# The end of a streamed cross attention: weighted sums, denominators and value biases in another order and on another engine

## The chip, the cores and the metric

The kernel runs on one core of a Trainium2 chip. The metric is the device time of one execution in microseconds. Before the change the median of three runs is 1160.88 us (1160.07 to 1163.15).

## What is computed

One block of a perceiver, all in float32 at its inputs and outputs: 512 tokens `x` of 512 numbers attend to 8192 context vectors, then to each other by linear attention, and then go through a feed-forward layer in simulated 8-bit arithmetic. Each part is added to `x`.

```python
def reference(x, ctx_1024, ...):
    # cross attention: 16 heads of 32, softmax over 8192 keys
    q = split_heads(layernorm(x) @ Wq + bq)
    k = split_heads(ctx_1024 @ Wk + bk)
    v = split_heads(ctx_1024 @ Wv + bv)
    z = softmax(q k^T / sqrt(32)) v
    x = x + merge_heads(z) @ Wo + bo
    # linear attention: 128 random features per head, elu + 1
    x = x + _L0_attn_ref(layernorm(x), w_qkv, proj_matrix, w_out, b_out)
    # feed-forward: 8-bit quantized products, exact gelu between
    x = x + _L0_ffn_ref(layernorm(x), W1, b1, W2, b2)
    return x
```

The change concerns the cross attention alone: the weighted sums of `v`, the denominators of the softmax, and the value bias `bv`, which is added after the division, since the weights of a softmax sum to 1.

## The kernel before

**Tiling.** The 8192 keys are taken in 16 blocks of 512. Heads are taken four at a time, so that four heads of 32 numbers fill 128 partitions; there are four such groups `g`. A block has four tiles `k` of 128 keys. A unit is one triple (block, g, k), and the loop at L784 goes through all 256 of them, in this order, 16 per block: the last block's are the units from `last_block` (240) on. They are numbered 0 to 15 below; unit 4 is the first of group 1, and so on.

**A unit's work.** `weights` (L723) makes the scores of four heads against 128 keys, four products on TensorE into `sc`, which takes four PSUM banks and has one buffer, and then the exponentials `ex` (128 x 2048) on ScalarE; `ex` has four buffers. So the scores of the next unit wait until ScalarE has read the last ones. `summed` (L748) adds the exponentials to a running sum `acc[:, g]` on VectorE, from which the denominators come at the very end. `weighted_sums` (L679) multiplies a unit's exponentials with the values, into a PSUM tile `av` which collects the four units of a group; the function that it returns adds that tile to `Z[:, g]` on VectorE after the fourth (L696), and does nothing after the others. The weighted sums run late: `late` holds the units whose exponentials are made and whose weighted sums are not.

**What else TensorE does.** Keys and values of the next block are made in small steps, kept in `queue` and issued by `ahead` between the units. In the last block what is left are keys of that block's own later groups (`pk`, L395), one product per unit, as long as there are any (to unit 10); their results get their bias on ScalarE (L401).

**The last block before the change** (L786 to L804). After a unit's scores and exponentials, VectorE gets the unit's addition to the running sum. In the second unit of a group (`k == 1`) the group before is finished (`finish`, L717): its denominators `dn` are a product of the running sum with ones (`sums`, L700), VectorE takes their reciprocal (`inverse`, L707), multiplies Z with it and adds the value bias (`divide`, L710). Then come the weighted sums of the unit before with their addition to Z, and then a step of the queue. Group 3's denominators are collected in another tile over its four units straight from the exponentials, and group 3's running sum gets no additions in this block. `av` and `dn` share two PSUM buffers (`ps_a`), which are handed on as they come free.

**Order.** Nearly every instruction goes through `in_order`, which keeps it in the program's order on its engine. Each engine takes its instructions one after the other, so an instruction that waits holds all behind it on that engine; engines wait for each other by semaphores.

**Behind the block** the output products `po` (L840) multiply Z with `Wo`, token tile by token tile: first groups 0 to 2 for two tiles, then group 3. Normalization, linear attention and the feed-forward layer follow.

Of the kernel before, what the change touches and what calls it, by code (L numbers as in the profile page):

```python
# [9 lines left out]
F32 = mybir.dt.float32  # L10
BF16 = mybir.dt.bfloat16
AF = mybir.ActivationFunctionType
ALU = mybir.AluOpType
# [4 lines left out]
P = 128  # L18
# [9 lines left out]
def network(  # L28
# [24 lines left out]
    nc = tc.nc  # L53
    S, E = x.shape
# [4 lines left out]
    NE = E // P  # L59
# [32 lines left out]
    def in_order(i):  # L92

        return tc.keep_in_program_order(i)
# [6 lines left out]
    def load_cols(src, n, name):  # L101
        t = const.tile([P, n], F32, name=name)
        nc.sync.dma_start(t, src)
        return t
# [6 lines left out]
    def place_w():  # L111
        return wpool.tile([P, NE, E], F32, name="w")

    def load_w(src, w=None):
        w = w or place_w()
        nc.sync.dma_start(w, src.rearrange("(c p) n -> p c n", p=P))
        return w
# [146 lines left out]
    with ExitStack() as actx:  # L264
# [5 lines left out]
        Z = aw.tile([P, NE, S], F32, name="Z")  # L270
        acc = aw.tile([P, NE, HG, S], F32, name="acc")
# [7 lines left out]
        bias = aw.tile([P, NE], F32, name="bias")  # L279

        rd = acc[:, :, 0, :]
# [28 lines left out]
        bv_sb = load_cols(bv, NE, "bv_sb")  # L310
# [238 lines left out]
        def ahead(n):  # L549
            for _ in range(n):  # L550
                cost, step = queue.pop(0)
                step()
                done[0] += cost
# [120 lines left out]
        ps_a = ctx.enter_context(tc.tile_pool(name="ps_a", bufs=2, space=PSUM))  # L674
        sctx = actx.enter_context(ExitStack())
        ps_s = sctx.enter_context(tc.tile_pool(name="ps_s", bufs=1, space=PSUM))
        av, late = {}, []

        def weighted_sums(b, g, k, ex):  # L679
            if k == 0:  # L680
                av[g] = ps_a.tile([P, S], F32, name="av")
            assert ("v", b, k, g // 2) in made
            for j in range(HG):
                in_order(nc.tensor.matmul(  # L684
                    av[g][ts(j, D), :], lhsT=vt[b][:, k, ds(g * P + j * D, D)],
                    rhs=ex[:, j, :], start=(k == 0), stop=(k == NC - 1),
                ))
            if k < NC - 1:
                return lambda: None
            ps = av.pop(g)  # L690

            def added():
                if b == first:
                    in_order(nc.vector.tensor_copy(Z[:, g, :], ps))
                else:
                    in_order(nc.vector.tensor_tensor(Z[:, g, :], Z[:, g, :], ps, ALU.add))  # L696

            return added

        def sums(dn, ex, start, stop):  # L700
            for j in range(HG):
                in_order(nc.tensor.matmul(
                    dn[ts(j, D), :], lhsT=ones_f, rhs=ex[:, j, :],
                    start=start, stop=stop,
                ))

        def inverse(g, dn):  # L707
            in_order(nc.vector.reciprocal(rd[:, g, :], dn))

        def divide(g):  # L710

            in_order(nc.vector.tensor_tensor(Z[:, g, :], Z[:, g, :], rd[:, g, :], ALU.mult))
            in_order(nc.vector.tensor_scalar(
                Z[:, g, :], Z[:, g, :], bv_sb[:, g : g + 1], None, ALU.add
            ))

        def finish(g):  # L717
            dn = ps_a.tile([P, S], F32, name="dn", tag="av")
            sums(dn, acc[:, g], True, True)
            inverse(g, dn)  # L720
            divide(g)

        def weights(b, g, k):  # L723

            assert ("k", b, g, k // 2) in made
            sc = ps_s.tile([P, HG, S], F32, name="sc")
            if exact:
                for j in range(HG):
                    in_order(nc.tensor.matmul(
                        sc[:, j, :], lhsT=ones_h[ds(j * D, 3), :],  # L730
                        rhs=mrow[ds(j * D, 3), g, :], start=True, stop=False,
                    ))
            for j in range(HG):
                rows = ts(j, D)
                in_order(nc.tensor.matmul(  # L735
                    sc[:, j, :], lhsT=kT[b][rows, g, ts(k, P)], rhs=qT[rows, g, :],
                    start=not exact, stop=True,
                ))
            ex = ap4.tile([P, HG, S], F32, name="ex")
            if exact:  # L740
                in_order(nc.scalar.activation(ex, sc, AF.Exp, scale=SCALE))
            else:
                in_order(nc.scalar.activation(  # L743
                    ex, sc, AF.Exp, bias=bias[:, g : g + 1], scale=SCALE
                ))
            return ex

        def summed(b, g, k, ex):  # L748
            if b == first and k == 0:
                in_order(nc.vector.tensor_copy(acc[:, g], ex))  # L750
            elif (b, g) != (total - 1, NE - 1):
                in_order(nc.vector.tensor_tensor(acc[:, g], acc[:, g], ex, ALU.add))  # L752
# [23 lines left out]
        def due(i):  # L776
            for (i0, c0), (i1, c1) in zip(marks, marks[1:]):
                if i <= i1:
                    return c0 + (c1 - c0) * (i - i0) // (i1 - i0)
            return c1  # L780
# [3 lines left out]
        for i, u in enumerate(units):  # L784
            ex = weights(*u)
            if i >= last_block:  # L786
                b, g, k = u
                summed(*u, ex)
                if k == 1 and g > 0:
                    finish(g - 1)  # L790
                if g == NE - 1:
                    if k == 0:
                        dn = ps_m.tile([P, S], F32, name="dn", tag="pt")
                    sums(dn, acc[:, g] if k == 0 else late[0][-1], k == 0, False)
                while late:
                    weighted_sums(*late.pop(0))()
                if queue:
                    ahead(1)
                if i == last_block + 2:

                    wo_sb, wv2_sb = load_w(Wo), place_w()
                    wk2_sb = load_w(w_qkv[:, E : 2 * E])
                    wq2_sb = load_w(w_qkv[:, :E])
                    load_w(w_qkv[:, 2 * E :], wv2_sb)  # L804
            elif i % 3 == 0 and i > 0:
                add = [weighted_sums(*late.pop(0)) for _ in range(3)]
                summed(*u, ex)
                for a in add:
                    a()
                if wq_steps:  # L810
                    wq_steps.pop(0)()
            else:
                upto = due(i + 1) if i % 3 == 2 else (due(i - 1) + due(i + 2)) // 2
                if i < 3:
                    upto = done[0] + 4
                while queue and done[0] < upto:
                    ahead(1)
                summed(*u, ex)
            late.append((*u, ex))
# [3 lines left out]
        inverse(NE - 1, dn)  # L823
        weighted_sums(*late.pop(0))()
        divide(NE - 1)

# [384 lines left out]
    for q in range(NF // 4):  # L1213
# [14 lines left out]
        for i in range(4):  # L1228
# [7 lines left out]
            if i % 2 == 1:  # L1236
                k = f // 2
# [49 lines left out]
@with_exitstack  # L1287
def perceiver_block(ctx: ExitStack, tc: tile.TileContext, **args):
    nc = tc.nc
    fate = ctx.enter_context(tc.tile_pool(name="fate", bufs=1))  # L1290
    wrong = fate.tile([1, 1], mybir.dt.int32, name="wrong")
    network(tc, False, wrong, **args)
    again = nc.values_load(wrong, min_val=0, max_val=1)
    with tc.If(again > 0):
        network(tc, True, None, **args)
# [50 lines left out]
```

## Time and profile before

| | us |
|---|---|
| median of three runs | 1160.88 |
| the profiled execution | 1161.99 |
| its span | 1160.1 |
| TensorE busy in the span | 1102.5 |
| VectorE busy | 929.6 |
| ScalarE busy | 630.7 |
| last block, from its first scores to the first output product | 936.93 to 996.11 |
| exponentials of one unit (L743), mean | 1.968 |
| reciprocal of 128x512 (L708), mean | 3.355 |
| value bias on VectorE (L713), mean | 0.487 |
| key bias on ScalarE (L401), mean | 0.688 |

The times of the profile count from the start of the span. PE is TensorE, PEld its weight loads, DVE VectorE, ACT ScalarE, SP the engine that issues most transfers. Matmuls are pipelined, so the length printed for one is longer than the distance from its start to the next one's; distances of starts say what it costs. The granted clock of TensorE is 1.00 in the whole last block.

### The profile page before, as it was taken

What the parts mean: (1) busy time and instruction counts of PE and PEld (TensorE: products, weight loads), DVE (VectorE), ACT (ScalarE), POOL (GpSimd) and SP (SyncE); (2) the same over time, 40 slices, a digit from 0 to 9 for tenths busy, and PEclk for the clock granted to TensorE, in tenths of its full rate; (3) what the DMA queues carried; (4) which work ended last, traced back from release to release, by engine and by line L of the source; (5) the groups of instructions that cost most, each with busy time, mean ns of one, the idle gap of its engine ahead of it and who ended that gap; (6) DMA issues with size and microseconds to landing.
All of it is one profiled execution on the core that took longest, in us unless ns stands there. A gap on an engine that the chain in (4) does not pass through costs nothing.

```text
span 1160.1 us, 15823 instructions
## 1 busy us (share of the span) xinstructions
PE 1102.5 (95%) x6793; PEld 524.5 (45%) x6793; DVE 929.6 (80%) x840; ACT 630.7 (54%) x419; POOL 138.0 (12%) x80
## 2 busy tenths in 40 slices
PE   5999999999999999999999999999999999999865
PEld 2334454444544544544544544545544422344332
DVE  2458899989888888888888888888888879656886
ACT  1044555456666666666665555555555565336353
POOL 2420203003203011203010202010100000000000
PEclk9999999999999999999999999999999999999987
DMA  7021212120202120202110101010100021030001
GB/s 254 1 73 44 85 55 73 55 81 13 89 29 67 53 64 28 91 28 64 55 46 10 37 1 38 1 37 1 37 37 1 1 74 37 37 146 1 1 1 39
DMA packets 24686, 54.59 MB, mean 47 GB/s; under 512 B 1952, under 2 KB 2464, under 8 KB 24352
## 3 DMA queue, kind: packets, MB, share of 16 engines
q1 hardware_dynamic: 24320, 52.97, 13.8%
q8 instruction: 55, 0.90, 0.3%
q10 hardware_dynamic: 288, 0.52, 0.1%
q14 instruction: 23, 0.19, 0.1%
HBM read 48.25 MB, written 5.24 MB: 46 GB/s over the span
## 4 chain that ended last, share of the span: by engine, by line
PE 83%; DVE 8%; issue 5%; ACT 4%; POOL 0%; DVEq 0%; POOLq 0%; ACTq 0%
PE pm L467 29%; PE sc L735 22%; PE av L684 18%; ACT ex L743 4%; DVE acc L752 2%; PE pk L395 2%; PE po L840 2%; PE pq L944 2%; PE pys L1253 1%; PE pq L122 1%; PE pv L876 1%; DVE unchanged L129 1%; PE pv L417 1%; DVE de L1044 1%; PE att L1034 1%
## 5 line engine op out<-in xcount | busy, mean ns | idle before, releaser
L743 ACT ACTIVATE ex<-sc,bias 128x2048 f32<-128x2048 f32 x256 | 503.8, 1968 | 406.0 <-PE sc L735 400.2
L752 DVE TENSOR_TENSOR acc<-acc,ex 128x2048 f32<-128x2048 f32 x248 | 587.0, 2368 | 78.1 <-ACT ex L743 75.9
L735 PE MATMUL sc<-qT,kT 32*128 32x512 f32 x2048 | 292.0, 640 | 5.3 <-ACT ex L743 4.8
L684 PE MATMUL av<-ex,vt 128*32 128x512 f32 x2048 | 239.5, 596 | 1.6 <-DVE Z L696 1.6
L735 PEld LDWEIGHTS sc<-qT,kT 32*128 32x128 f32 x2048 | 79.9, 182 | 140.6 <-ACT ex L743 124.4
L684 PEld LDWEIGHTS av<-ex,vt 128*32 128x32 f32 x2048 | 57.2, 109 | 169.6 <-issue 166.2
L380 POOL TENSOR_TENSOR tt<-ct 128x512 f32<-128x512 f32 x30 | 47.7, 1591 | 614.0 <-DMA ct<-in_ctxT 606.8
L467 PE MATMUL pm<-w,tt 128*128 128x256 f32 x480 | 118.3, 389 | 0.3 <-ACT vt L488 0.3
L467 PE MATMUL pm<-tt,w 128*128 128x256 f32 x448 | 110.5, 389 | 0.2 <-DVE kT L478 0.2
L467 PEld LDWEIGHTS pm<-w,tt 128*128 128x128 f32 x480 | 87.4, 190 | 44.8 <-issue 31.0
L467 PEld LDWEIGHTS pm<-tt,w 128*128 128x128 f32 x448 | 81.5, 190 | 42.5 <-issue 26.4
L475 DVE TENSOR_TENSOR vt<-vt,pm 128x512 f32<-128x512 f32 x105 | 70.6, 685 | 30.1 <-PE pm L467 22.3
L467 PE MATMUL pm<-w,ct 128*128 128x256 f32 x360 | 91.8, 391 | 0.0
L467 PE MATMUL pm<-ct,w 128*128 128x256 f32 x336 | 85.6, 391 | 4.9 <-DVE kT L478 3.9
L467 PEld LDWEIGHTS pm<-w,ct 128*128 128x128 f32 x360 | 65.0, 189 | 36.4 <-issue 29.2
L467 PEld LDWEIGHTS pm<-ct,w 128*128 128x128 f32 x336 | 60.7, 189 | 38.4 <-issue 25.5
L380 POOL TENSOR_TENSOR tt<-ct,tt 128x512 f32<-128x512 f32 x30 | 75.2, 2508 | 1.2
L475 DVE TENSOR_TENSOR kT<-kT,pm 128x512 f32<-128x512 f32 x56 | 38.2, 682 | 15.0 <-PE pm L467 9.2
L478 DVE SCALAR_TENSOR_TENSOR kT<-pm,bk_sb,kT 128x256 f32<-128x256 f32 x84 | 36.5, 476 | 5.5 <-PE pm L467 5.2
L696 DVE TENSOR_TENSOR Z<-Z,av 128x512 f32<-128x512 f32 x60 | 40.8, 679 | 0.0
L966 ACT ACTIVATE er<-feat 128x1024 f32<-128x1024 f32 x32 | 30.2, 1028 | 8.9 <-PE feat L987 6.7
L970 DVE SCALAR_TENSOR_TENSOR f<-er 128x1024 f32<-128x1024 f32 x16 | 19.4, 1219 | 15.1 <-ACT er L966 15.1
(172 smaller groups left out, 598.3 us busy)
## 6 DMA issues: line engine op xcount, KB each, us to landing
ct<-in_ctxT SPq DMA_DIRECT2D x16, 1024.0 KB, 5.7
wraw<-in_W1T SPq DMA_DIRECT2D x16, 512.0 KB, 3.8
wraw<-in_W2T SPq DMA_DIRECT2D x16, 512.0 KB, 3.6
wd<-wquant SPq DMA_DIRECT2D x16, 256.0 KB, 2.4
w_q<-wd SPq DMA_DIRECT2D x2, 2048.0 KB, 10.6
w<-in_w_qkv SPq DMA_DIRECT2D x3, 1024.0 KB, 5.1
w<-in_Wq SPq DMA_DIRECT2D x1, 1024.0 KB, 8.4
w<-in_Wk SPq DMA_DIRECT2D x1, 1024.0 KB, 10.2
```

Source lines behind the costliest of these rows:

```text
L380: in_order(nc.gpsimd.tensor_tensor(tt[b][:, i], x, y, ALU.subtract))
L395: in_order(nc.tensor.matmul(part[0], lhsT=wk_sb[:, c, ts(g, P)], rhs=ct[b][:, c, :], start=(c == 0), stop=(c == NE - 1),))
L467: in_order(nc.tensor.matmul(st["ps"][n][:, m, :], lhsT=lhsT[:, k, ts(m, P)], rhs=rhs[:, k, :], start=k == 0, stop=k == 1,))
L475: in_order(nc.vector.tensor_tensor(dst, src, ps, ALU.add))
L478: in_order(nc.vector.scalar_tensor_tensor(dst[:, m, :], ps[:, m, :], bk_sb[:, 2 * i + m : 2 * i + m + 1], src[:, m, :], ALU.add, ALU.add,))
L684: in_order(nc.tensor.matmul(av[g][ts(j, D), :], lhsT=vt[b][:, k, ds(g * P + j * D, D)], rhs=ex[:, j, :], start=(k == 0), stop=(k == NC - 1),))
L696: in_order(nc.vector.tensor_tensor(Z[:, g, :], Z[:, g, :], ps, ALU.add))
L735: in_order(nc.tensor.matmul(sc[:, j, :], lhsT=kT[b][rows, g, ts(k, P)], rhs=qT[rows, g, :], start=not exact, stop=True,))
L743: in_order(nc.scalar.activation(ex, sc, AF.Exp, bias=bias[:, g : g + 1], scale=SCALE))
L752: in_order(nc.vector.tensor_tensor(acc[:, g], acc[:, g], ex, ALU.add))
L840: in_order(nc.tensor.matmul(po, lhsT=lhsT[:, c, ts(t, P)], rhs=w[:, c, :], start=(c == 0), stop=(c == NE - 1),))
L966: in_order(nc.scalar.activation(er[-1][:, d].rearrange("p a n -> p (a n)"), ps[h], function))
```

## The change

It has three parts, all in the last block.

- The weighted sums of the unit before, with their addition to Z, and the step of the queue now come ahead of the unit's addition to the running sum. On TensorE nothing but their place against the denominators changes by it; on VectorE an addition to Z stands ahead of a running sum behind which it stood.
- The denominators of the group before come behind the unit's weighted sums and its step of the queue, no longer ahead of them. The reciprocal and the multiplication follow the unit's running sum on VectorE, as before.
- The value bias is taken out of `divide` into a new function `biased`. For groups 0 to 2 it is issued in the fourth unit of the next group and runs on ScalarE, as an activation with the identity function; for group 3 it stays on VectorE, behind the multiplication.

```diff
         def divide(g):
-
             in_order(nc.vector.tensor_tensor(Z[:, g, :], Z[:, g, :], rd[:, g, :], ALU.mult))
-            in_order(nc.vector.tensor_scalar(
-                Z[:, g, :], Z[:, g, :], bv_sb[:, g : g + 1], None, ALU.add
-            ))
-
-        def finish(g):
-            dn = ps_a.tile([P, S], F32, name="dn", tag="av")
-            sums(dn, acc[:, g], True, True)
-            inverse(g, dn)
-            divide(g)
+
+        def biased(g):
+
+            if g < NE - 1:
+                in_order(nc.scalar.activation(
+                    Z[:, g, :], Z[:, g, :], AF.Identity, bias=bv_sb[:, g : g + 1]
+                ))
+            else:
+                in_order(nc.vector.tensor_scalar(
+                    Z[:, g, :], Z[:, g, :], bv_sb[:, g : g + 1], None, ALU.add
+                ))
...
             if i >= last_block:
                 b, g, k = u
-                summed(*u, ex)
-                if k == 1 and g > 0:
-                    finish(g - 1)
+
+
                 if g == NE - 1:
...
                     weighted_sums(*late.pop(0))()
                 if queue:
                     ahead(1)
+                if k == 1 and g > 0:
+                    dn_g = ps_a.tile([P, S], F32, name="dn", tag="av")
+                    sums(dn_g, acc[:, g - 1], True, True)
+                summed(*u, ex)
+                if k == 1 and g > 0:
+                    inverse(g - 1, dn_g)
+                    divide(g - 1)
+                if k == 3 and g > 0:
+                    biased(g - 1)
...
         inverse(NE - 1, dn)
         weighted_sums(*late.pop(0))()
         divide(NE - 1)
+        biased(NE - 1)
```

## The prediction, made before the changed kernel had run

> **What bounds the kernel now.** I read the page's busy shares first, then the chain that ended last, then the waits of the last block alone, and at the end the timeline of that block, engine by engine. The block's sixteen units are numbered 0 to 15 here, four to a group; unit 0's scores start at 936.93 us, and the output products behind the block start at 996.11 us.
>
> ```profile
> PE 1102.5 (95%) x6793; PEld 524.5 (45%) x6793; DVE 929.6 (80%) x840; ACT 630.7 (54%) x419; POOL 138.0 (12%) x80
> PE 83%; DVE 8%; issue 5%; ACT 4%; POOL 0%; DVEq 0%; POOLq 0%; ACTq 0%
> ```
>
> TensorE is busy 95% of the span and is 83% of the chain: what takes it work or waiting off is worth time one for one, and what is done for the other engines is worth nothing unless TensorE or the loop scores - exponentials - scores waits for it. The change touches only the last 60 us before the output products, so these decide. The chain in order of time, units 4 to 6 (start, length, what):
>
> ```profile
> 951.46 1.18 PE sc L735 x8
> 952.64 0.02 issue
> 952.66 1.98 ACT ex L743
> 954.64 0.02 issue
> 954.66 2.29 DVE acc L752
> 956.96 0.61 DVE Z L696
> 957.57 0.04 issue
> 957.61 1.07 PE av L684 x8
> 958.68 1.06 PE pk L395 x2
> 959.73 1.07 PE sc L735 x8
> ```
>
> In unit 5 the chain leaves TensorE: it goes through the exponentials of unit 4, their running sum and the addition of group 0's weighted sums to Z, and only then do the weighted sums of group 1 start. It does the same at 969.33 to 972.28 (unit 9). The same stretch in the timeline:
>
> ```profile
> 954.68 1.14 PE L735 MATMUL sc<-qT,kT 32*128 32x512 f32 x8
> 955.76 1.07 PE L702 MATMUL dn<-acc,ones_f 128*32 128x512 f32 x8
> 957.61 1.07 PE L684 MATMUL av<-ex,vt 128*32 128x512 f32 x8 [0.79 <-DVE Z L696]
> 958.61 1.13 PE L395 MATMUL pk<-ct,w 128*128 128x512 f32 x2
> 959.66 1.14 PE L735 MATMUL sc<-qT,kT 32*128 32x512 f32 x8
> 960.10 3.35 DVE L708 RECIPROCAL acc<-dn 128x512 f32<-128x512 f32 x1
> 960.87 1.97 ACT L743 ACTIVATE ex<-sc,bias 128x2048 f32<-128x2048 f32 x1 [3.01 <-PE sc L735]
> 963.49 0.69 DVE L712 TENSOR_TENSOR Z<-Z,acc 128x512 f32<-128x512 f32 x1
> 964.22 0.49 DVE L713 TENSOR_SCALAR Z<-Z,bv_sb 128x512 f32<-128x512 f32 x1
> ```
>
> An ordinary unit takes 3.23 us from scores to scores (962.89, 966.12, 969.35): 1.21 us from the scores' start to the exponentials', 1.97 us of exponentials, 0.04 us to the next scores. Unit 5 takes 4.98 us (954.68 to 959.66), unit 9 too (969.35 to 974.33), unit 13 takes 3.79 us (984.02 to 987.80). The waits of the block put 1.6 us in two pieces of 0.8 us to the addition to Z.
>
> **The change part by part.** *Additions to Z ahead of the running sums.* Group 0's last weighted sums start at 952.53 us (unit 4) and VectorE's running sum before them ends at about 953.73, so the addition can run 953.75 to 954.43 instead of 956.87 to 957.55, and unit 4's running sum, ready at 954.63, still starts on time. In group 1 it stands behind the sums of units 6 and 7, as before, and comes at about 968.9 to 969.6; nobody on TensorE hangs on that one at the weighted sums any more: by the order of buffers in the changed program the weighted sums of group 1 take a PSUM buffer free since unit 0, those of group 2 the one that the reciprocal of group 0 left (963.45), and only the denominators of group 1, three products later (about 971.7), wait for that addition. Both 0.79 us waits go. In unit 0, the addition now waits for three units' weighted sums (to about 940.8) and the running sum slips from 940.14 to about 941.5, ending 943.8; the next one starts when its exponentials end (944.95), which hides it.
>
> *Denominators behind the unit's other products.* Unit 5 becomes scores, weighted sums, keys, denominators, scores. Start to start, from rows: scores to 128x32 products 1.07 us (945.00 to 946.07), those to keys 1.00 us (957.61 to 958.61), keys to whatever follows 1.06 us (973.27 to 974.33), 128x32 products to scores 0.97 us (986.83 to 987.80). Sum 4.10 us against 4.98: 0.88 us less. The unseen step is keys to denominators; its nearest row is keys to scores (1.05 to 1.12 us), and the last step lies between 0.87 (denominators on denominators) and 1.0 us, so 3.99 to 4.20 us. The old order without its wait would be 4.98 - 0.85 = 4.13 us by starts, or about 4.0 us by pitches: the new order itself gains nothing. Twice 0.88 us: 1.76 us (1.56 to 1.98). In unit 13 there is no keys' product left and no wait before: 1.07 + 0.87 + 0.87 + 0.97 = 3.78 us against 3.79, no gain. The reciprocal of group 2 starts at TensorE's pace, 1.1 us after its denominators, so later within the unit; VectorE has nothing else there (idle 1.66 us before it now), and Z of group 2 is wanted only in the third output product.
>
> [...]
>
> *Three bias additions on ScalarE.* VectorE loses 3 x 0.49 us (L713). Its additions to Z no longer hold TensorE, so the time it saves is worth 0; if they still did, group 1's bias alone would be on the path, 0.4 us. ScalarE gets three. The nearest rows, the same operation with PSUM as source (L401, L346), take 0.69 us; a 128x1024 one in SBUF (L211) takes 1.23 us, which bounds it from above. They stand behind the exponentials of units 7, 11 and 15. There ScalarE waits 1.26 us for the next scores, which hides 0.69 us; the upper bound leaves 0.03. What they bring is a wait: they need VectorE's product with the reciprocal, and the next exponentials queue behind them. That product ends at 964.18 us for group 0 (nothing before it moves); unit 7's exponentials end at about 965.2 and unit 8's start at 966.45, so it could be 1.6 us later. For group 1, VectorE runs the sums of units 6 and 7 (from 964.22, 2.39 us apart), the addition (968.9), the sums of 8 and 9 (969.6, 971.9), the reciprocal (974.1) and the product (977.5 to 978.2); unit 12's exponentials start at 980.3 us: 1.4 us to spare. The third lies behind the last exponentials, ahead of the table load, whose function is wanted 10 us later. Cost 0.
>
> [...]
>
> *A by-product.* In the changed program four exponentials (units 8, 9, 12, 13) wait for the scores in a separate instruction ahead of them, as they now know of VectorE's sums through the bias. The nearest row is the addition to xs (L846): the one with such a wait starts 0.11 us after its product's end (1002.50), the one without 0.04 us (1010.15). I take 0.07 us, 0 to 0.1. It counts only where ScalarE's loop sets the pace, units 8 and 12: 0.14 us.
>
> *Behind the block* the order is the old one, and neither SP's nor GpSimd's queue changes. The last weight load (977.55, released by the last keys' product) moves up with it; the output products, normalizations and the rest are released by TensorE and VectorE and shift as a whole.
>
> Sum: 1.76 - 0.14 = 1.62 us. The profiled execution took 1161.99 us (span 1160.1 and 1.9 around it), so 1160.4; it is 1.1 us above the median of the runs shown, 1160.88, from which I predict 1159.3 us. By the bounds of the parts the gain is 1.4 to 2.0 us, 1158.9 to 1159.5.
>
> **The rivals.** *The gain does not reach the end* (1160.9). From 1090 us on, TensorE is idle by stretches (busy 0.74 of 5 us at 1100, none at 1125) and the granted clock falls to 0.50 at 1105 and 1130 to 1140. Where the fall lies against the stages is not set by this block; 1.6 us more of the tail at half clock costs 0.8 us, as much less saves it, and both such places together could take the gain. For it: the three runs shown lie 3.1 us apart. Against: nothing in the chain behind 996 us has a fixed date.
>
> *ScalarE waits for VectorE* (slower). The place is the bias after units 7 and 11. From 1.6 and 1.4 us of lateness of VectorE on, each further us delays the next exponentials by one. One running sum (2.29 us) more ahead of each reciprocal costs 0.7 + 0.9 us and just eats the gain (1160.9); it decides from about 2.3 us on, and two sums (4.58 us) cost 3.0 + 3.2 us: 1165.5. For it: VectorE is busy 14.1 of 14.67 us in units 5 to 8. Against: it loses a bias per group, and the product's date follows from rows.
>
> *TensorE packs tighter.* If the denominators fit beside the exponentials, units 5, 9 and 13 take 3.23 us: 3 x 3.23 against 4.98 + 4.98 + 3.79 gives 4.1 us less, 1156.8. Against: four products at 0.87 us or more already take 3.5.
>
> **How the numbers follow.** My forecast has 0.75, the lost gain 0.12, ScalarE's wait 0.07 (0.05 of it past the bound), the tighter packing 0.06. Some 0.3% (3.5 us) is what a measurement here can tell from no change: the forecast (0.14%) and the lost gain are the same by it. Faster by more: the tighter packing and a lucky tail, 0.08; slower 0.05; the same 0.87. The range goes from the tighter packing, 1157.0, over the forecast and the lost gain with 1 us of scatter on it, to 1161.9.
>
> **What would show it.** Right: in unit 5 and unit 9 no wait of the weighted sums for Z, scores 4.1 us apart; the bias on ScalarE at 0.6 to 0.75 us in a gap before unit 8 and unit 12; output products at about 994.5 us. Wrong: exponentials of unit 8 or 12 released by VectorE's product, denominators waiting for the addition to Z, or the span not following the output products' start.

## The result and the profile after

The changed kernel is faster by 0.16%: the ratio of its runs to those of the kernel before is 0.9984, with a 95% interval of 0.9976 to 0.9992 (12 runs each; medians 1160.2 and 1161.5 us). In a later comparison, beside other experiments, it was 0.9978 (0.9969 to 0.9987). In microseconds that is a gain of 1.9 (0.9 to 2.8) and 2.6 (1.5 to 3.6); the forecast was 1.6. The forecast time, 1159.3 us, counted from the 1160.88 us of three runs; over twelve runs the kernel before has a median of 1161.5 us.

The page of the changed kernel, busy shares and the chain's shares by engine:

```profile
PE 1101.9 (95%) x6790; PEld 523.9 (45%) x6793; DVE 926.1 (80%) x837; ACT 632.5 (55%) x422; POOL 138.2 (12%) x80
PE 84%; DVE 7%; ACT 4%; issue 4%; POOL 0%; DVEq 0%; ACTq 0%; POOLq 0%
```

TensorE's work is the same; one per cent of the chain went from VectorE to TensorE. The chain in order of time, units 4 to 6, as it was shown of the kernel before:

```profile
949.98 1.14 PE sc L736 x8
951.12 1.00 PE av L684 x8
952.11 1.06 PE pk L395 x2
953.17 0.04 issue
953.20 1.14 PE sc L736 x8
954.35 0.99 PE av L684 x8
955.34 1.06 PE pk L395 x2
956.40 1.00 PE dn L702 x8
957.39 1.07 PE sc L736 x8
```

The chain no longer leaves TensorE in unit 5: exponentials, running sum and addition to Z are gone from it. The timeline of the changed kernel over the same stretch follows; in brackets stands how long the engine was idle ahead of a row, and what ended that (`<-`):

```profile
952.18 0.69 DVE L696 TENSOR_TENSOR Z<-Z,av 128x512 f32<-128x512 f32 x1
953.18 2.29 DVE L753 TENSOR_TENSOR acc<-acc,ex 128x2048 f32<-128x2048 f32 x1 [0.32 <-ACT ex L744]
...
953.20 1.14 PE L736 MATMUL sc<-qT,kT 32*128 32x512 f32 x8
954.27 1.06 PE L684 MATMUL av<-ex,vt 128*32 128x512 f32 x8
955.27 1.12 PE L395 MATMUL pk<-ct,w 128*128 128x512 f32 x2
956.33 1.06 PE L702 MATMUL dn<-acc,ones_f 128*32 128x512 f32 x8
957.32 1.14 PE L736 MATMUL sc<-qT,kT 32*128 32x512 f32 x8
...
962.00 0.69 DVE L711 TENSOR_TENSOR Z<-Z,acc 128x512 f32<-128x512 f32 x1
...
963.62 0.71 ACT L716 ACTIVATE Z<-Z,bv_sb 128x512 f32<-128x512 f32 x1
965.05 1.97 ACT L744 ACTIVATE ex<-sc,bias 128x2048 f32<-128x2048 f32 x1 [0.71 <-PE sc L736]
```

The addition to Z ends at 952.87 us, ahead of the running sum of unit 4, which still starts 0.03 us after its exponentials, as before the change. Weighted sums, keys and denominators follow each other without a wait, and unit 5 takes 4.12 us from scores to scores instead of 4.98. The bias on ScalarE finds its operand 0.9 us early and is done 0.7 us before the next exponentials.

What the bias brings to these exponentials is a small wait. The chain of the changed kernel shows it in unit 8, and behind the dots, for comparison, an ordinary start in unit 10. `ACTq` is ScalarE's queue, in which a separate instruction waits for the scores:

```profile
964.96 0.02 issue
964.99 0.02 ACTq L744
965.00 0.05 issue
965.05 1.98 ACT ex L744
...
975.60 0.02 issue
975.63 1.98 ACT ex L744
```

With the separate instruction the exponentials start 0.09 us after the scores' end, without it 0.03 us.

From its first scores to the first output product, the block takes 57.58 us (935.45 to 993.03) instead of 59.18 us: 1.60 us less. The spans of the two profiles differ by 2.7 us; the other 1.1 us lie outside the block. Ahead of it, where the programs are the same, the block begins between 935.45 and 937.65 us in the eleven profiles of this study; the stretch behind it takes 162.7 to 164.5 us. Within the block equal units agree to 0.01 us from profile to profile. So the experiments are read by units and by the block, and whole times say only whether that arrives.

### The profile page after: what moved, and what is told of

Same layout as the page of the kernel before. It is cut to its first block, busy times and chain, and to the rows that moved or that the text cites. A ratio compares the mean times of both kernels' runs of the same rounds, so it can differ in the third digit from the quotient of the medians.

```text
span 1157.4 us, 15820 instructions
## 1 busy us (share of the span) xinstructions
PE 1101.9 (95%) x6790; PEld 523.9 (45%) x6793; DVE 926.1 (80%) x837; ACT 632.5 (55%) x422; POOL 138.2 (12%) x80
## 4 chain that ended last, share of the span: by engine, by line
PE 84%; DVE 7%; ACT 4%; issue 4%; POOL 0%; DVEq 0%; ACTq 0%; POOLq 0%
PE pm L467 29%; PE sc L736 23%; PE av L684 19%; ACT ex L744 4%; PE pk L395 2%; PE po L850 2%; PE pq L954 2%; DVE acc L753 2%; PE pys L1263 1%; PE pv L886 1%; PE pq L122 1%; DVE unchanged L129 1%; PE pv L417 1%; DVE de L1054 1%; PE att L1044 1%
```

## The experiments

From scores to scores, in us; the other units take 3.22 to 3.23 us in all of them, but unit 0, which takes 4.84, and unit 15, which takes 5.08 to 5.09 to the first output product.

| kernel | unit 5 | unit 8 | unit 9 | unit 12 | unit 13 | block |
|---|---|---|---|---|---|---|
| before | 4.98 | 3.23 | 4.98 | 3.23 | 3.78 | 59.18 |
| changed | 4.12 | 3.29 | 4.12 | 3.29 | 3.78 | 57.58 |
| part 1 alone | 3.98 | 3.23 | 3.98 | 3.23 | 4.35 | 57.76 |
| part 2 alone | 4.12 | 3.23 | 4.66 | 3.23 | 3.78 | 58.01 |
| part 3 alone | 4.98 | 3.29 | 4.97 | 3.30 | 3.78 | 59.30 |
| parts 1 and 2 | 4.11 | 3.23 | 4.12 | 3.22 | 3.79 | 57.46 |
| parts 1 and 3 | 3.98 | 3.28 | 3.98 | 3.29 | 3.78 | 57.30 |
| denominators spread | 3.23 | 3.23 | 3.98 | 3.23 | 3.78 | 56.44 |

**Part 1 alone: weighted sums ahead of the running sum.** Against the kernel before:

```diff
-                summed(*u, ex)
                 if k == 1 and g > 0:
-                    finish(g - 1)
+                    dn_g = ps_a.tile([P, S], F32, name="dn", tag="av")
+                    sums(dn_g, acc[:, g - 1], True, True)
...
                 if queue:
                     ahead(1)
+                summed(*u, ex)
+                if k == 1 and g > 0:
+                    inverse(g - 1, dn_g)
+                    divide(g - 1)
```

A change of tiling mode means here that the shape which the rows print for TensorE's products (`32*128`, `128*32`, `128*128`) changes from one product to the next. In the profile before, products of the same `128*32` follow each other at 0.86 to 0.88 us (starts at 985.09, 985.97 and 986.83).

> The kernel before with the first part alone: weighted sums, addition to Z and the queue's step ahead of the running sum; denominators still ahead of the weighted sums, value biases on VectorE. My theory (the wait of the weighted sums for the addition to Z is the whole gain): that wait goes in units 5 and 9, and with no change of tiling mode between denominators and weighted sums a unit is 1.07 + 0.87 + 1.00 + 1.06 = 4.00 us; the block from its first scores to the first output product takes 59.18 - 2 x 0.98 = 57.2 us, 2.0 us less than before and 0.4 us less than with all three parts (57.58). Rival (the late place of the denominators is what gains): the wait moves to another product and the block stays at 59.2 us.

Units 5 and 9 take 3.98 us, 0.02 less than expected, but the block is 0.56 us longer than expected: unit 13 takes 4.35 us, 0.57 more than before. The timeline of that unit in this kernel:

```profile
979.09 4.68 DVE L752 TENSOR_TENSOR acc<-acc,ex 128x2048 f32<-128x2048 f32 x2
...
982.19 1.14 PE L735 MATMUL sc<-qT,kT 32*128 32x512 f32 x8 [0.23 <-ACT ex L743]
...
983.83 1.06 PE L702 MATMUL dn<-acc,ones_f 128*32 128x512 f32 x8 [0.50 <-DVE acc L752]
984.71 1.04 PE L702 MATMUL dn<-ex,ones_f 128*32 128x512 f32 x8
...
985.57 1.04 PE L684 MATMUL av<-ex,vt 128*32 128x512 f32 x8
```

Two running sums stand behind the reciprocal and the bias of group 1 on VectorE and end at 983.77 us. TensorE, now 2 us earlier, comes to group 2's denominators at about 983.3 and waits 0.50 us for them. A wait was removed and another, hidden until then, took part of its place. The whole runs do not show the block's 1.4 us (a ratio of 0.9988): the ratio is 0.9997 (0.9988 to 1.0007).

**Part 2 alone: denominators behind the other products.** Against the kernel before, `finish(g - 1)` is moved:

```diff
                 summed(*u, ex)
-                if k == 1 and g > 0:
-                    finish(g - 1)
...
                 if queue:
                     ahead(1)
+                if k == 1 and g > 0:
+                    finish(g - 1)
```

> The kernel before with the second part alone: denominators behind the weighted sums and the queue's step, running sums where they were, biases on VectorE. My theory: the weighted sums take another PSUM buffer by this order and wait no more, in unit 5 the denominators' own wait for the addition to Z (ends 957.55) is just covered (they are ready at 957.8): 4.12 us; in unit 9 that addition ends at 972.2 and the denominators, ready at 971.6, wait 0.6 us: about 4.8 us. Block 59.18 - 0.86 - 0.2 = 58.1 us, 1.1 us less than before. Rival (the second part carries the whole gain): both units 4.1 us, block 57.5 us. Rival (it does nothing without the first): block 59.2 us.

Unit 5 takes 4.12 us as expected, and unit 9 takes 4.66, 0.14 less than expected. The wait in unit 9, in the timeline of this kernel:

```profile
969.95 1.12 PE L395 MATMUL pk<-ct,w 128*128 128x512 f32 x2
970.81 0.68 DVE L696 TENSOR_TENSOR Z<-Z,av 128x512 f32<-128x512 f32 x1
971.55 0.64 PE L702 MATMUL dn<-acc,ones_f 128*32 128x512 f32 x4 [0.47 <-DVE Z L696]
```

The first 0.86 us of the gain need no earlier addition to Z: by the order of the requests alone the weighted sums get a PSUM buffer (one of the two that TensorE's products `av` and `dn` are written to) that is free: in unit 5 they start at 955.15 us, while the addition to Z ends at 956.95. In unit 9 the denominators have to wait for that addition instead, as it stands behind three running sums; only with part 1 does this go. The ratio of whole runs is 1.0002 (0.9992 to 1.0013), where the block's 1.17 us would give 0.9990.

**Part 3 alone: biases on ScalarE.** Against the kernel before, `biased` as in the change, called behind the queue's step:

```diff
+                if k == 3 and g > 0:
+                    biased(g - 1)
```

> The kernel before with the third part alone: the value biases of groups 0 to 2 on ScalarE behind the exponentials of units 7, 11 and 15. My theory: VectorE's saved 0.49 us is followed by a running sum that waits for its exponentials anyway, so units 5 and 9 keep 4.98 us; units 8 and 12 grow by 0.06 us by the separate wait: block 59.3 us, 0.1 us more than before. Rival (VectorE holds the block up, and its relief is part of the gain): unit 9 shrinks by 0.4 us, block 58.8 us.

As expected: units 5 and 9 are as before, units 8 and 12 are 0.06 us longer, the block 0.12 us longer (59.30; whole runs 1.0008, 0.9999 to 1.0018). VectorE's relief alone is worth nothing in the block.

**Parts 1 and 2, without part 3.** Against the changed kernel, the bias back on VectorE behind the multiplication:

```diff
                     divide(g - 1)
-                if k == 3 and g > 0:
                     biased(g - 1)
```

(with `biased` on VectorE for every group).

> The changed kernel without the third part: value biases back on VectorE right behind the multiplication. My theory: units 5 and 9 stay at 4.12 us without a wait, units 8 and 12 go from 3.29 back to 3.23 us as no exponentials wait in a separate instruction: block 57.58 - 0.12 = 57.46 us, 1.7 us less than before. Rival (the biases on ScalarE are part of the gain): block 57.9 us or more, by 0.4 us in unit 9.

As expected, to the hundredth: 57.46 us, and units 8 and 12 back at 3.23. The ratio is 0.9985 (0.9975 to 0.9994). So in the whole change the biases on ScalarE cost 0.12 us and give nothing. What costs is the separate wait: the changed kernel's ScalarE waits 1.32 us ahead of the exponentials of units 9 and 13, this one's 1.26 us.

**Parts 1 and 3, without part 2.** Against the changed kernel, denominators ahead of the weighted sums:

```diff
                 b, g, k = u
+                if k == 1 and g > 0:
+                    dn_g = ps_a.tile([P, S], F32, name="dn", tag="av")
+                    sums(dn_g, acc[:, g - 1], True, True)
...
                 if queue:
                     ahead(1)
-                if k == 1 and g > 0:
-                    dn_g = ps_a.tile([P, S], F32, name="dn", tag="av")
-                    sums(dn_g, acc[:, g - 1], True, True)
```

> Parts one and three without the second: denominators ahead of the weighted sums, biases on ScalarE. With part one alone unit 13 took 4.35 us, as group 2's denominators waited 0.50 us for unit 11's running sum on VectorE. My theory: without group 1's bias (0.4 us) VectorE ends that sum 0.4 us earlier and the separate waits of units 8 and 12 make the products 0.12 us later, so the wait nearly goes: units 5 and 9 at 3.98 us, 8 and 12 at 3.29, unit 13 at 3.8 to 3.9 us; block 57.3 us. Rival (the wait is of another cause): unit 13 stays at 4.35 us, block 57.9 us.

Unit 13 is back at 3.78 us and the block takes 57.30 us, less than with all three parts:

```profile
978.87 2.29 DVE L753 TENSOR_TENSOR acc<-acc,ex 128x2048 f32<-128x2048 f32 x1
...
981.80 1.06 PE L702 MATMUL dn<-acc,ones_f 128*32 128x512 f32 x8
```

The second of the two running sums ends at 981.16 us, 0.64 us ahead of the denominators, which do not wait. Counted from the block's start VectorE ends it 1.0 us earlier than with part 1 alone, not the 0.4 us expected: by then two value biases of some 0.5 us, group 0's and group 1's, are off its path. So the 0.50 us wait of part 1 alone came from the time at which VectorE was done, and here the bias on ScalarE has a value: 0.57 us, less 0.12 for the separate waits. Parts 2 and 3 each cure that wait; with both, one is superfluous. The ratio of whole runs is 0.9983 (0.9973 to 0.9993).

**Biases one unit earlier.** Against the changed kernel:

```diff
-                if k == 3 and g > 0:
+                if k == 2 and g > 0:
                     biased(g - 1)
```

> The changed kernel with the value biases on ScalarE one unit earlier, behind the exponentials of units 6, 10 and 14. My theory (the rival of the prediction in which ScalarE waits for VectorE, priced): the multiplication with the reciprocal ends at 962.69 us by the trace of the changed kernel, ScalarE would start unit 7's exponentials at 961.76, so the bias holds them to 963.35, 1.6 us late; the same after unit 10 (1.6 us) and, less, after unit 14 (0.4 us). Block 57.58 + 3.6 = 61.2 us, 2.0 us longer than before the change. Rival (ScalarE has spare time everywhere, so the place of three short instructions does not matter): block 57.6 us.

Unit 7 takes 4.82 us in place of 3.23, and unit 11 takes 4.87: 1.6 us each, as expected, and 0.4 us came at the end of the block. The chain of this kernel shows how the delay is handed on:

```profile
958.79 3.28 DVE acc L708
962.07 0.02 issue
962.09 0.70 DVE Z L711
962.79 0.02 issue
962.82 0.02 ACT Z L716
962.84 0.60 issue
963.44 1.96 ACT ex L744
965.40 0.04 issue
965.45 1.18 PE sc L736 x8
```

Reciprocal, multiplication, bias, exponentials, scores: a bias of 0.72 us that waited on ScalarE until 962.82 us held the exponentials behind it, which start at 963.44. But the block took 63.81 us, 2.6 more than expected: 2.3 of them lie in unit 12, which took 5.59 us in place of 3.29, and 0.3 in unit 13. The timeline on TensorE:

```profile
977.15 1.06 PE L684 MATMUL av<-ex,vt 128*32 128x512 f32 x8
980.95 2.09 PE L736 MATMUL sc<-qT,kT 32*128 32x512 f32 x8 [2.74 <-ACT ex L744]
```

And the busy time of the engines by stretches of the same kernel. The columns are the stretch and its length; the busy time and, in brackets, the instructions of PE, PEld, DVE, ACT and POOL; then the granted clock (the share of its full clock that TensorE was given), the busy share of the DMA engines and the GB/s:

```profile
974.00:978.00 4.00, 3.96 (x26) 0.84 (x26) 3.97 (x3) 2.65 (x2) 0.00 (x0) 1.00 0.15 22
978.00:981.00 3.00, 0.26 (x8) 0.05 (x4) 2.56 (x3) 2.58 (x2) 0.00 (x0) 0.89 0.84 321
981.00:983.00 2.00, 2.00 (x12) 0.50 (x13) 2.00 (x1) 0.00 (x0) 0.00 (x0) 0.50 0.00 0
983.00:985.00 2.00, 2.00 (x16) 0.56 (x16) 0.23 (x1) 1.83 (x1) 0.00 (x0) 0.50 0.00 0
```

TensorE waited 2.74 us here, against 1.62 us in unit 7, as unit 11 has no keys left to fill the wait with. The granted clock fell to 0.50, where it stayed until about 987 us, and eight passes of scores took 2.09 us instead of 1.14. The whole runs are slower than before by 0.18% (1.0018, 1.0008 to 1.0029), 2.1 us; that is less than the 4.6 us by which the block is longer in this profile, and why is not shown. The same kernel was profiled once more:

> The kernel with the biases one unit earlier, once more. In its first profile unit 12 took 5.59 us instead of 3.29, at a granted clock of 0.50 from about 980 to 987 us, behind a stretch of 2.74 us in which TensorE waited for ScalarE. If the clock falls on every such stretch, unit 12 takes 5.6 us again and the block 63.8 us; if it depends on where the stretch falls against something that is not fixed to the program, it may stay at 1.00, unit 12 takes 3.3 us and the block 61.5 us.

There the stretch was 2.73 us, the clock fell again, to 0.56 and 0.59 over 982 to 984 and 984 to 986 us and 1.00 from 986 on; unit 12 took 4.56 us and the block 62.50, between the two values expected. The clock fell in both profiles, for a longer and for a shorter time.

**Denominators spread.** This is the version that the runs point to: as parts 1 and 2, but group 0's denominators go to unit 11, where TensorE has time, and group 1's stand ahead of the weighted sums. Against the kernel with parts 1 and 2:

```diff
+                if k == 1 and g == 2:
+                    dn_g = ps_a.tile([P, S], F32, name="dn", tag="av")
+                    sums(dn_g, acc[:, g - 1], True, True)
                 if g == NE - 1:
...
-                if k == 1 and g > 0:
+                if k == 1 and g == 3:
                     dn_g = ps_a.tile([P, S], F32, name="dn", tag="av")
                     sums(dn_g, acc[:, g - 1], True, True)
+                if i == last_block + 11:
+                    dn_0 = ps_m.tile([P, S], F32, name="dn", tag="pt")
+                    sums(dn_0, acc[:, 0], True, True)
                 summed(*u, ex)
-                if k == 1 and g > 0:
+                if i == last_block + 12:
+                    inverse(0, dn_0)
+                    divide(0)
+                    biased(0)
+                if k == 1 and g > 1:
```

> The changed kernel without ScalarE's biases (as in the run without the third part), with group 0's denominators moved from unit 5 to unit 11, where TensorE waits 1.09 us for ScalarE, in a PSUM buffer of the keys, their reciprocal behind unit 12's addition to Z; group 1's denominators ahead of the weighted sums (no change of tiling mode between), group 2's behind them. My theory (in the block only TensorE's work in units without slack costs time): unit 5 takes 3.23 us, unit 9 3.98 us, unit 11 stays at 3.23 us, unit 13 at 3.78 us; block 59.18 - 1.75 - 1.00 = 56.4 us, 2.8 us less than before and 1.1 us less than with the change: some 0.24% faster than before. Rival (VectorE's reciprocals, crowded behind unit 12, delay group 3's): the block is 56.4 us, but the output products wait for Z and the gain is lost behind it.

The block takes 56.44 us: unit 5 an ordinary 3.23, unit 9 3.98, unit 13 3.78, and unit 11 carries group 0's denominators and keeps 3.23, from its scores to those of unit 12:

```profile
973.50 1.14 PE L731 MATMUL sc<-qT,kT 32*128 32x512 f32 x8
...
975.46 1.04 PE L702 MATMUL dn<-acc,ones_f 128*32 128x512 f32 x8
...
976.73 1.14 PE L731 MATMUL sc<-qT,kT 32*128 32x512 f32 x8 [0.23 <-ACT ex L739]
```

TensorE's wait for ScalarE there shrank from 1.09 us in the changed kernel to 0.23 us. The stretch behind the block (163.34 us) is within that of the others. The ratio to the kernel before is 0.9968 (0.9957 to 0.9979). Against the changed kernel the block is 1.14 us shorter, and the whole runs of the same comparison lean the same way (medians 1158.1 and 1160.0 us), though the intervals of the two ratios overlap.

**The changed kernel again,** beside these three:

> The changed kernel itself beside the others on one chip: 0.15% faster than before, its block 57.58 us as in its first profile, while the stretch ahead of the block, the same in all these kernels, moves by up to 1 us from profile to profile.

Its block took 57.58 us again, and the ratio is the 0.9978 given above. Its block began 2.2 us later in the span than in the first profile, where up to 1 us was expected.

## Why the prediction was right

- *What bounds.* Two waits of TensorE for the addition to Z were named as all there was to gain. Both are gone in the trace, and the kernel that kept them (part 3 alone) gained nothing. Parts 1 and 2 alone each remove the weighted sums' wait, so its cause, the order on VectorE and the PSUM buffer that was asked for, is shown from both sides.
- *Unit lengths.* 4.10 us were summed for units 5 and 9, 4.12 were measured. Keys to denominators, the step without a row, took 1.06 us as taken; denominators to scores took 0.99 in place of 0.97. For the old order without its wait the prediction gave two figures, 4.13 and about 4.0 us; part 1 alone measures it, 3.98, so the second holds.
- *The order costs.* The rows before the change give 0.86 to 0.88 us between products of one shape and 0.97 to 1.07 us where the shape changes; from these follows, as an estimate, some 0.1 us for a change more. The units take 4.12 us with the denominators behind the keys and 3.98 us with them beside the weighted sums, where the shape changes once less, so it was 0.14 us. That is what the order costs; by what TensorE loses it, no run shows.
- *The separate waits.* 0.07 us were taken for each from a row on VectorE, 0.06 us measured. Sum: 1.62 us forecast for the block, 1.60 measured. The whole runs are a weaker proof: their interval, 0.9 to 2.8 us, would have held other sums too.
- *ScalarE's biases.* 0.71 us measured against 0.69 taken, hidden as forecast. One unit earlier they delay units 7 and 11 by 1.6 us each, as the rival of ScalarE's wait gives with one us for each us that VectorE is late. In the whole change the additions were better left on VectorE, by 0.12 us, because of the separate waits and not of the length of the instruction; with parts 1 and 3 alone they were not, as there the bias on ScalarE gains 0.46 us.
- *Incomplete.* "In unit 13 there is no keys' product left and no wait before ... no gain" is true of the whole change but missed what the place does there: with the waits gone, the denominators in the old place and the bias on VectorE, group 2's denominators come 0.50 us too early for VectorE, and 0.57 us would be lost. What VectorE's bias delays was worked out only for the times of the old order. Likewise "the time it saves is worth 0" holds for VectorE's relief in the whole change and for part 3 alone, but not beside part 1 without part 2. So the change holds two cures for one wait, and of the two the denominators' new place is the dearer: without it the block takes 57.30 us instead of 57.58.
- *The rivals.* That the gain is lost behind the block is ruled out by the two comparisons of whole runs, whose intervals leave out zero. The fall of the granted clock behind the block did move against the stages: taken as a fall to 0.50, by the mean clocks it began at some 1098.6 us instead of 1103.9 (0.86 over 1095 to 1100 us, before the change 0.89 over 1100 to 1105), 5.3 us earlier, and the product that ends TensorE's wait there starts 3.1 us earlier (1100.54 instead of 1103.64). No exponentials waited for VectorE's product in the changed kernel: both were 0.7 us behind the bias's end. TensorE did not pack tighter: units 5 and 9 take 4.12 us, not 3.23. The 0.3% that the prediction took as the least difference to be told was too much: with twelve runs each the interval reaches 0.08% to either side.
- *Behind the block.* That the rest shifts as a whole could be shown only to its own scatter (162.7 to 164.5 us), which is as large as the gain. The output products start at 993.03 us, not at the 994.5 forecast, because the block began 1.48 us earlier in this profile; that part is chance. Why whole runs of part 1 alone and of part 2 alone read about 0.1% slower than their blocks say is not settled; nothing in their profiles shows it.

## What to carry to other kernels

When a wait is taken away, everything behind it comes earlier, and the operands that used to be early have to be placed in time anew: here a second wait of 0.5 us lay just behind the first. Where an engine is the bound, look for units in which it waits for something else. Work moved there can be free, as group 0's denominators are in unit 11: the move took unit 5 from 4.11 to 3.23 us, as much again as the reordering had brought there (4.98 to 4.11). A short instruction moved to an engine with spare time hides there only while its operand is ready before its place in the queue (0.9 us before it in the change; one unit earlier it held the exponentials back, by 1.6 us in units 7 and 11), and it can still lengthen the start of others, here by 0.06 us in two units.

## What the runs showed of the hardware that was not expected

In the kernel with the biases one unit earlier TensorE waited 2.74 us in one profile and 2.73 us in the other, between stretches in which it was busy, and the granted clock fell there: to 0.50 in the first, to a mean of 0.56 and 0.59 over two stretches of 2 us in the second. The fall cost 2.6 us and 1.3 us, up to nearly as much again as the wait. If the clock stood at 0.50 for as long as it was down, then by its means over the stretches it was down for 6.8 us in the first profile (0.89 over 978 to 981, 0.50 to 987, 0.92 to 988) and for 3.4 us in the second (0.56 over 982 to 984, 0.59 to 986). By the same estimate the fall began at 980.3 us in the first profile, while TensorE still waited (until 980.95), and at 982.2 us in the second, 0.9 us after TensorE had gone on (981.33). So with the same program and the same wait the fall cost twice as much in one profile as in the other; what sets its start and its length is not shown. At shorter waits (1.62 us in the first of these profiles, 1.09 us in unit 11 of the changed kernel) the clock stayed at 1.00; a wait between 1.62 and 2.73 us is in none of the profiled blocks.

With the separate instruction for the wait ahead of them, exponentials started 0.06 us later, by the chain and the waits of 1.32 and 1.26 us above. Here moving an operation to another engine caused this in instructions that were not touched: with the bias on ScalarE units 8 and 12 take 3.29 us, without it 3.23. That what an engine already knows of the others decides which waits are left is a reading of the program; the traces do not show it.
